# Two x loads moved to SyncE's queue, bands issued in order of use, a softmax planned later, five more evictions on ScalarE

## The chip, the cores and the metric

The kernel runs on one core of one Trainium2 chip. The metric is the device time in microseconds (us) of one execution. The core has five engines with a queue each: TensorE (PE, matmuls; PEld is its weight load), VectorE (DVE), ScalarE (ACT), GpSimd (POOL) and SyncE (SP). SP, ACT and POOL issue DMAs; "SPq" and "ACTq" are the queues of SP and ACT in the profile.

## The reference

All is float32. x has the shape 4 images x 256 channels x 64 x 64. First layer: attention over a dilated 7 x 7 neighbourhood; second layer: whitening of groups of 64 channels over all pixels of all images.

```python
k = conv(x, w1, rhs_dilation=(2, 2), padding=6) + b1          # 7x7, 256 -> 128
k = conv(k, w2, 1x1) + b2                                      # 128 -> 49
attn = softmax(k, axis=1)                                      # 49 weights per pixel
xp = pad(x, 6)
shifts = stack([xp[:, :, 2*u:2*u+64, 2*v:2*v+64] for u in range(7) for v in range(7)], 1)
y = einsum('bkchw,bkhw->bchw', shifts, attn)
# whitening: per group of 64 channels, mean and Sigma over all images and pixels,
# five Newton steps P = 1.5 P - 0.5 P^3 Sigma_N, then out = (P sqrt(rTr)) (y - mean) * weight + bias
```

## The kernel before, in words

**Storage.** x is kept in SBUF as "slots": slot k holds the rows of one parity of image k // 2 (k = 2b + parity). There are five SBUF buffers for eight slots. Slot 0 and 1 are loaded first in an order that suits the convolution of image 0 and later again in the order "halves" that the rest uses. `read_x` (L140) issues the four DMAs of one slot, 512 KB each, in runs of 32 floats; `load_x` (L158) calls it, or takes a copy arranged in DRAM beforehand (`ahead`, slots 5 to 7, one DMA of 2 MB). Results y overwrite x in the slots; `move` spills finished slots to DRAM and loads slots 5 to 7 in their place.

**Logits.** The two convolutions are merged and computed by a Toom-Cook scheme: seven row evaluations `br` and seven column points in three banks (`BANKS`). `conv_step(k, i)` runs the matmuls of bank i of row k (L599; 96, 80 and 32 of them), prepares the next row's inputs xh, rb, ct on DVE (L347, L350, L354) and fetches weights wr: by ACT's queue from DRAM (`wr<-gd`, L419), or, the first time a row is used, built from kept sums that SP loads (L428, L445) and stored again (L481). `direct_start`, `direct_inf` and `direct0` are the direct products (L765). Interpolation on DVE gives the logits.

**Softmax.** `soft(b, pc)` handles image b and column parity pc in two steps. Each turns half of the logits by PE transposes (L999); DVE takes maxima (L1035, L1036) and ACT does 16 exps with sums (L1039); the second step scales and shuffles on DVE (L1014 to L1023, four shuffles at L987) and marks the pair in `soft_done`. The second step is called after the next conv step (`rest_of`). The last image uses `softmax_rows` (L1060 to L1069), with more of it on DVE.

**Weighted sum.** The sum over the 49 shifts is done in 16 units n = 4b + k, one per image, row parity h and column parity pc. For one n: `move_terms(n)` (L1085) copies the softmax terms into a staging tile zt (11 copies, on ACT at L1117, for the last image on DVE at L1129) and writes it to DRAM scratch `sd` with eight DMAs (L1136, on POOL; four of n = 12 on SP). It returns without doing anything when the softmax of that pair isn't in `soft_done`. `load_band(n, half)` (L1162) reads from sd, by SP, the banded matrices of one half of the image: two DMAs `band` (L1173, column halves h0 and h1, 242 KB each) and two small ones `bandz` (L1184) for the edge between the halves. `first_half(n)` and `second_half(n)` turn x blocks by PE transposes (L1218, evicted by ACT at L1232 and L1241, in the tail by DVE), multiply them with the bands (L1269) in the order of `PIECES` (half 0 uses the mains first and the edge last; half 1 the edge first), and call `store_y` (L1287, L1289), which evicts the sum to the slot: the two channel halves cc = 0 and 1 both on ACT, but in the tail (`tail` set, from second_half(10) on) cc = 1 on DVE. `turn_y` transposes y (L1300, evicted at L1308), `moments` accumulates the statistics (L1321).

**Order of the work.** PE's order is the program's. A tile scheduler orders the other queues by its own estimates and priorities, subject to data dependencies and to manual ones: a "NoSync" dependency only fixes the order of two instructions, a "Sync" one makes the later wait. The weighted sums of image b are laid between the conv steps of image b + 1 or later. `plan(b, j, f)` puts f into eighth j of image b's conv steps (j of 8 and more goes on into the next image), in the order in which the calls were made, and `gap(b, j)` runs them. For image 1 the units start in eighth 2 of image 2: `first_half(4)` is planned for (2, 2), `second_half(4)` for (2, 3), `first_half(5)` for (2, 4), and so on; for image 2 `first_half(8)` comes at (3, 3). The softmaxes of images 1 and 2 are planned for eighths 0 and 1 of the next image, those of image 0 run at fixed places. `first_half(n)` itself calls `move_terms(n + 1)` and `load_band(n + 1, 0)` at its end; `second_half(n)` calls `bands(n + 1)`, which does for n + 1 (and the terms of n + 2) whatever is possible by then and hasn't been done.

**The x loads in question.** Slot 1 is loaded again (its second arrangement) after `load_band(0, 1)`, and slot 4 from the plan of eighth (1, 2); both on POOL's queue, eight DMAs in all, with a Sync dependency on the last DMA of band (0, 1) (`behind`, `first_band`).

Of the kernel before, what the change touches and what calls it, by code (L numbers as in the profile page):

```python
# [32 lines left out]
def kernel(  # L33
# [29 lines left out]
    nc = tc.nc  # L63
    B, C, H, W = x.shape
    P = 128
    NCC = C // P
# [3 lines left out]
    R = KS // 2  # L70
    SH, SW = H // 2, W // 2
    CR = P // SW
    NCH = SH // CR
    HALF = SH // 2
# [11 lines left out]
    TR8, TC = 8, SW // 2  # L86
    WS = 22
    TROWS = TR8 + R
    ROW0 = (0, TR8 - R, 2 * TR8, 3 * TR8 - R)
    COLS = ((0, TC + R), (TC - R, SW))  # L90
    LS = 2 * KS * WS
    RS = TC * (LS - 1) + WS
    HS = SH * RS
# [15 lines left out]
    def tp():  # L109
        return ps_tp.tile([P, 512], F32, tag="tp", name="tp")  # L110
# [18 lines left out]
    slots = {}  # L129
    store = []  # L130

    def halves(t):

        return t.rearrange("p c r w -> p c (r w)").rearrange(
            "p c (h r w) -> p c h r w", h=2, r=SH
        )

    ahead = {}

    def read_x(o, k, queue):  # L140
        b, pr = divmod(k, 2)
        dmas = []
        for cc in range(NCC):
            src = x[b, cc * P : (cc + 1) * P].rearrange("c (r two) w -> c r two w", two=2)
            for h in range(2):
                dmas.append(
                    queue.dma_start(o[:, cc, h], src[:, :, pr, h * SW : (h + 1) * SW])  # L147
                )
        return dmas

    def arrange_x(k, queue):

        ahead[k] = dram.tile([P, NCC * SH * W], F32, name=f"ahead{k}")
        return read_x(
            ahead[k].rearrange("p (c h r w) -> p c h r w", c=NCC, h=2, w=SW), k, queue
        )

    def load_x(s, k, queue):  # L158
        slots[k] = store[s]
        if k in ahead:  # L160
            return [queue.dma_start(store[s].rearrange("p c r w -> p (c r w)"), ahead[k])]
        return read_x(halves(store[s]), k, queue)

    s01 = ctx.enter_context(tc.tile_pool(name="s01", bufs=1))
    for s in range(2):
# [17 lines left out]
    t = tp()  # L183
# [3 lines left out]
    t = tp()  # L187
# [5 lines left out]
    for k in range(2):  # L193
        t = ps_cv.tile([P, 512], F32, name=f"cv{k}")
# [19 lines left out]
    for c0, c1 in ((0, 3), (3, 6), (6, 9), (9, 11), (11, 13)):  # L214
        c0, c1 = c0 * CB, min(c1 * CB, P)
# [32 lines left out]
    for k, c0 in enumerate(range(0, P, CB)):  # L248
        n = min(CB, P - c0)
        t = cv_buf[k % 2]  # L250
# [15 lines left out]
    for k0 in range(0, KT, TB):  # L266
        n = min(TB, KT - k0)
        t = tp()
# [622 lines left out]
    def behind(dmas, name):  # L891
        for dma in dmas:
            tc.add_manual_dep(
                dma.ins,
                name,
                mybir.DependencyInfo(mybir.DependencyClass.Sync, mybir.DependencyReason.DATA),
                reason="behind",
            )
# [14 lines left out]
    for s in range(2, 4):  # L913
        behind(load_x(s, s, nc.gpsimd), quiet)
# [10 lines left out]
    for k in range(5, 8):  # L925
        behind(arrange_x(k, nc.gpsimd), turn[0])
# [14 lines left out]
    )  # L941
    row_eval(0, 5, [rb[0], rb[1], xrs[5]])
    load_x(0, 0, nc.gpsimd)
    col_interp(0, 1)
    col_interp(0, 2)
# [23 lines left out]
    band = bpool.tile([P, 4, 2, TROWS, WS], F32, name="band")  # L969
    bandz = bpool.tile([P, 2, R, SW], F32, name="bandz")  # L970
# [56 lines left out]
    def softmax(b, pc):  # L1027

        nm = f"{b}_{pc}"
        mx = work.tile([P, NCH, 2], F32, tag="mx", name=f"mx_{nm}")  # L1030
        d = new_terms(b, pc)
        s = work.tile([P, 2, NCH], F32, tag="s", name=f"s_{nm}")
        for hf, t in enumerate(turned_logits(b, pc)):
            m = mx[:, NI * hf : NI * (hf + 1)]
            nc.vector.tensor_reduce(m, t[:, :, :, :KT], AX.X, ALU.max)  # L1035
            nc.vector.tensor_scalar(m, m, -1.0, None, ALU.mult)  # L1036
            for i in range(NI * hf, NI * (hf + 1)):
                for h in range(2):
                    nc.scalar.activation(  # L1039
                        d[:, h, i], t[:, i % NI, h, :KT], AF.Exp,  # L1040
                        bias=mx[:, i, h : h + 1], accum_out=s[:, h, i : i + 1],
                    )
            if hf == 0:
                yield
        for h in range(2):
            scale_terms(nm, h, d[:, h], s[:, h])
        shuffle(d.rearrange("p h i (u v) -> p (h i u) v", u=KS))
        soft_done.update((b, pc, h) for h in range(2))
# [23 lines left out]
        soft_done.add((b, pc, h))  # L1072

    terms, moved, loaded = {}, set(), set()
    written, soft_done, moved_by, first_band = [], set(), {}, []

    MOVES = [(0, 0, 4), (2, 0, 2), (2, 2, 2)]
    MOVES += [(s, j, 1) for s in (1, 3) for j in range(CR)]
# [72 lines left out]
    def bring_back(after):  # L1151

        for k in back:
            dma = nc.sync.dma_start(slots[k].rearrange("p a r w -> p (a r w)"), spill[k])
            tc.add_manual_dep(
                dma.ins,
                after.ins.name,
                mybir.DependencyInfo(mybir.DependencyClass.NoSync, mybir.DependencyReason.DATA),
                reason="bring_back",
            )  # L1160

    def load_band(n, half):  # L1162

        if (n, half) in loaded or n not in moved:
            return
        loaded.add((n, half))
        D = sd[n % 2][:]
        base = lambda t, h: (
            h * HS + TR8 * t * RS + (ROW0[t] - TR8 * t + R) * WS + COLS[h][0] - h * TC + R
        )  # L1170
        t0 = 2 * half
        for h in range(2):
            nc.sync.dma_start(  # L1173
                band[:, t0 : t0 + 2, h].rearrange("p t r w -> p t (r w)"),
                bass.AP(
                    tensor=D.tensor,
                    offset=D.offset + base(t0, h),
                    ap=[[LS - 1, P], [base(t0 + 1, h) - base(t0, h), 2], [1, TROWS * WS]],
                ),
            )  # L1180
        e = CR * half + (R if half else 0)
        for h in range(2):
            c0, c1 = COLS[h]
            dma = nc.sync.dma_start(  # L1184
                bandz[h * 64 : (h + 1) * 64, half, :, c0:c1],
                bass.AP(
                    tensor=D.tensor,
                    offset=D.offset + h * HS + (HALF - CR * half) * RS + e * WS + c0 - h * TC + R,
                    ap=[[LS - 1, 64], [WS, R], [1, c1 - c0]],
                ),  # L1190
            )
        if (n, half) == (4 * B - 1, 1):
            bring_back(dma)
        if (n, half) == (0, 1):
            first_band.append(dma.ins.name)
            behind(load_x(1, 1, nc.gpsimd), *first_band)

    blocks = {}

    tail, ahead_xb = [], []  # L1200
# [5 lines left out]
    def where(n):  # L1206

        b, h, pc = place(n)
        return slots[2 * b + h], pc
# [69 lines left out]
    def store_y(n, half):  # L1279
        yt, pc = where(n)  # L1280
        ps = y_ps.pop((n, half))
        for cc in range(NCC):
            o = halves(yt)[:, cc, :, half * HALF : (half + 1) * HALF, bass.ds(pc, TC, 2)]
            i = ps[:, cc].rearrange("p r (h c) -> p h r c", h=2)
            with tc.high_priority():
                if tail and cc:
                    nc.vector.tensor_scalar(o, i, pivot[:, cc : cc + 1], None, ALU.add)  # L1287
                else:
                    last = nc.scalar.activation(o, i, AF.Identity, bias=pivot[:, cc : cc + 1])  # L1289
        return last  # L1290
# [70 lines left out]
    def first_half(n):  # L1361
# [23 lines left out]
        weighted_sum(n, 0, 3)  # L1385
        weighted_sum(n, 0, 4)
        move_terms(n + 1, store_y(n, 0))
        half_done.add(n)
        load_band(n + 1, 0)
        if last is not None:  # L1390
            moments(last, 1)
# [5 lines left out]
    def bands(n, after=None):  # L1397

        move_terms(n, after)
        if n - 1 in half_done:  # L1400
            load_band(n, 0)
        if n - 1 in done:
            load_band(n, 1)
            move_terms(n + 1, after)
# [28 lines left out]
    def plan(b, j, *what):  # L1433
        todo.setdefault((b + j // NPC, j % NPC), []).extend(what)
# [3 lines left out]
    def soft(b, pc):  # L1438
        steps = softmax(b, pc)

        def step():
            with tc.high_priority() if pc == 0 else nullcontext():
                next(steps, None)

        step()
        if b == 0:
            step()
            if pc == 0:
                bands(0)
        else:  # L1450
            rest_of.append(step)
# [18 lines left out]
                    plan(b + 1, 3 + j, hs[j])  # L1470
    for b in range(B - 1):
        for j in range(2) if b else ():
            plan(b + 1, j, lambda b=b, j=j: soft(b, j))

    plan(1, 2, lambda: behind(load_x(4, 4, nc.gpsimd), *first_band))

    def gap(b, j):
        for f in todo.pop((b, j), ()):
# [2 lines left out]
    for b in range(1, B):  # L1481
# [13 lines left out]
        j, at, whole = 0, 0, sum(c for c, _ in steps)  # L1495
# [39 lines left out]
    n = 4 * last_b  # L1535
# [140 lines left out]
    n = [0]  # L1676
# [15 lines left out]
    for b in (3, 2, 1, 0):  # L1692
        for cc in range(NCC):
            for q in range(0, SH // TR, 2):
# [31 lines left out]
                for k in range(2):  # L1726
                    for i in (G0, G1):
                        o = i if k == 0 else (G1 if i is G0 else G0)
# [45 lines left out]
```

## Time and profile before

| | |
|---|---|
| time before, median of 3 runs | 729.38 us (725.12 to 730.21) |
| the profiled execution, its own time | 729.77 us |
| its span, first to last instruction | 727.8 us |
| mean granted clock of TensorE | 0.976 |
| PE busy | 687.1 us, 94% of the span |
| PEld, DVE, ACT, POOL busy | 543.5, 585.8, 341.5, 131.2 us |
| ACT L1289, y to slot, x53 | 0.735 us median of one |
| DVE L1287, y to slot, x11 | 0.751 us median of one |
| POOL L147, x load, x20 | 512 KB each, 7.5 us to landing (median) |
| SP L1173, band, x64 | 242 KB each, 3.2 us to landing (median) |
| POOL L1136, sd<-zt, x124 | 77 KB each, 3.0 us to landing (median) |

A line of the page's groups or of the timeline reads: source line, engine, operation, output<-inputs by the names of the program, shape, count, times. "Granted clock" is TensorE's clock as a share of full speed. A wait is written "who <- whom", with the sum in us, how often, and the longest. The chain of waits is the sequence of work and waits that ended last. The conv steps fill roughly 20 to 570 us, the weighted sums of the last image 570 to 660, the whitening matrix 660 to 673, and its application with the output stores the rest.

### The profile page before, as it was taken

How to read it: one execution, taken by the hardware profiler on the slowest of the kernel's cores; microseconds unless marked ns; L12 is line 12 of the kernel's file. 1: busy time of each engine (PE TensorE's matmuls, PEld its weight loads, DVE VectorE, ACT ScalarE, POOL GpSimd, SP SyncE). 2: the span in 40 equal slices, each digit the busy share in tenths (PEclk: the TensorE clock that was granted, in tenths of full speed). 3: DMA queues.
4: the chain of work that ended last, by engine and by line, in shares of the span. 5: the costliest groups of instructions: out<-in, count | busy, mean ns of one | idle time of the engine just before them, and what ended most of it. 6: DMA issues, size and time to landing. Idle time of an engine off the chain costs nothing.

```text
span 727.8 us, 19131 instructions
## 1 busy us (share of the span) xinstructions
PE 687.1 (94%) x7728; PEld 543.5 (75%) x7728; DVE 585.8 (80%) x1284; ACT 341.5 (47%) x954; POOL 131.2 (18%) x190
## 2 busy tenths in 40 slices
PE   6999999999998999998999999989999987997996
PEld 1449553377997998787999988889999877995231
DVE  3799998995796889999896699999969778325575
ACT  1423330133764565556563653646546533442564
POOL 0002625612361020002220200021302032200000
PEclk9999999999998999999999999999999999997998
DMA  8942999912897385226594760262733254463598
GB/s 324 233 122 94 240 386 216 228 30 56 220 239 208 115 261 198 92 63 166 170 308 132 235 203 2 62 178 81 194 103 66 59 126 97 108 247 145 237 361 326
DMA packets 78720, 126.09 MB, mean 173 GB/s; under 512 B 36471, under 2 KB 59112, under 8 KB 77480
## 3 DMA queue, kind: packets, MB, share of 16 engines
q1 hardware_dynamic: 60488, 64.84, 28.2%
q0 software_dynamic: 12096, 41.77, 21.7%
q10 hardware_dynamic: 6048, 18.27, 8.0%
q8 instruction: 61, 1.00, 0.6%
q14 instruction: 27, 0.22, 0.1%
HBM read 78.78 MB, written 52.36 MB: 180 GB/s over the span
## 4 chain that ended last, share of the span: by engine, by line
PE 69%; DVE 19%; ACT 5%; DMA 4%; issue 1%; SPq 0%; ACTq 0%; DVEq 0%
PE cv L599 21%; PE y L1269 10%; PE cv L765 9%; PE acc L765 8%; PE tp L1714 4%; PE tp L1300 4%; PE sig L1321 3%; PE tp L1218 3%; DMA band<-sd 3%; PE cv L253 2%; DVE pv L354 2%; DVE zz L354 2%; DVE d L987 1%; DVE xh L354 1%; DVE rb L347 1%
## 5 line engine op out<-in xcount | busy, mean ns | idle before, releaser
L599 PE MATMUL cv<-xh,wr 128*49 128x128 f32 x4160 | 232.4, 273 | 2.1 <-DMA wr<-gd 2.1
L599 PEld LDWEIGHTS cv<-xh,wr 128*49 128x49 f32 x4160 | 226.1, 124 | 5.8 <-issue 3.4
L1136 POOL DMA_DIRECT2D sd<-zt x124 | 65.3, 533 | 333.2 <-ACT zt L1117 272.7
L1269 PE MATMUL y<-band,xb 128*128 128x209 f32 x480 | 104.2, 349 | 7.1 <-DMA band<-sd 6.9
L1269 PEld LDWEIGHTS y<-band,xb 128*128 128x128 f32 x480 | 83.7, 196 | 8.2 <-DMA band<-sd 7.3
L610 ACT COPY pv<-cv 113x486 f32<-113x486 f32 (+2 forms) x60 | 25.9, 431 | 90.0 <-PE cv L599 83.0
L1308 ACT COPY yt<-tp 128x256 f32<-128x256 f32 x128 | 45.3, 377 | 41.7 <-PE tp L1300 40.8
L1300 PE MATMUL tp<-ident,slot 128*128 128x128 f32 x256 | 53.5, 306 | 8.7 <-DVE slot L1287 6.0
L354 DVE SCALAR_TENSOR_TENSOR pv<-pv 113x162 f32<-113x162 f32 x176 | 52.8, 321 | 4.2 <-ACT pv L610 3.4
L1300 PEld LDWEIGHTS tp<-ident,slot 128*128 128x128 f32 x256 | 41.4, 205 | 17.1 <-DVE slot L1287 6.7
L1218 PE MATMUL tp<-ident,slot 128*128 128x128 f32 x256 | 49.0, 305 | 3.3 <-ACT yt L1308 2.0
L1289 ACT ACTIVATE slot<-y,pivot 128x512 f32<-128x512 f32 x53 | 36.5, 736 | 25.7 <-PE y L1269 25.6
L147 POOL DMA_DIRECT2D slot<-in_x_dram x20 | 33.9, 1696 | 64.1 <-issue 50.5
L1218 PEld LDWEIGHTS tp<-ident,slot 128*128 128x128 f32 x256 | 38.6, 206 | 8.5 <-ACT xbz L1241 2.4
L1117 ACT COPY zt<-d 32x112 f32<-32x112 f32 (+2 forms) x132 | 38.3, 290 | 13.2 <-DVE d L987 11.3
L354 DVE SCALAR_TENSOR_TENSOR xh<-ct 128x512 f32<-128x512 f32 x40 | 26.7, 693 | 17.4 <-PE cv L599 17.3
L1232 ACT COPY xb<-tp 128x256 f32<-128x256 f32 x96 | 33.3, 375 | 14.2 <-PE tp L1218 13.4
L1321 PE MATMUL sig<-yt 128*64 128x65 f32 x1024 | 37.8, 228 | 0.0
L1321 PEld LDWEIGHTS sig<-yt 128*64 128x64 f32 x1024 | 33.3, 140 | 5.6 <-issue 4.0
L1039 ACT ACTIVATE d<-tp,mx 128x49 f32<-128x49 f32 x96 | 27.5, 322 | 20.9 <-DVE mx L1036 18.1
L765 PE MATMUL acc<-slot,tap 128*49 128x256 f32 (+7 forms) x224 | 34.7, 468 | 0.0
L765 PEld LDWEIGHTS acc<-slot,tap 128*49 128x49 f32 x224 | 16.2, 123 | 17.9 <-issue 15.5
(242 smaller groups left out, 1116.6 us busy)
## 6 DMA issues: line engine op xcount, KB each, us to landing
out_dram<-out SPq DMA_DIRECT2D x32, 512.0 KB, 3.6
band<-sd SPq DMA_DIRECT2D x64, 242.0 KB, 3.2
slot<-in_x_dram POOLq DMA_DIRECT2D x20, 512.0 KB, 7.5
sd<-zt POOLq DMA_DIRECT2D x124, 77.0 KB, 3.0
wr<-gd ACTq DMA_DIRECT2D x14, 588.0 KB, 5.5
wr<-gd ACTq DMA_DIRECT2D x14, 490.0 KB, 5.2
ahead<-in_x_dram POOLq DMA_DIRECT2D x12, 512.0 KB, 7.5
spill<-slot POOLq DMA_DIRECT2D x3, 2048.0 KB, 10.4
```

The lines of the kernel that those rows point to most:

```text
L147: queue.dma_start(o[:, cc, h], src[:, :, pr, h * SW : (h + 1) * SW])
L354: return in_turn(STT(o, a, f, b, ALU.mult, ALU.add))
L599: nc.tensor.matmul(o, wv[:, sc, sr, cc], xv[bc][:, h * NCC + cc], start=(j == 0), stop=(j == len(terms) - 1), skip_group_check=True,)
L765: nc.tensor.matmul(ps[h * HB : h * HB + KT, :, o0:o1], w[v][:, cc], rhs, start=(j == 0 and k == 0), stop=(j == len(order) - 1), skip_group ...
L1117: ins = nc.scalar.copy(o, i)
L1136: dma = queue.dma_start(bass.AP(tensor=D.tensor, offset=D.offset + h * HS + g * RS, ap=[[LS, TC], [CR * RS, NCH], [1, KS * WS]],), zt[p0 : ...
L1218: nc.tensor.transpose(t[:, cc * P : (cc + 1) * P], tile_of(xt, cc, t8, h, pc), ident)
L1269: nc.tensor.matmul(ps[:, cc, q0 : q0 + nq, c0:c1], xb[:, cc * P : (cc + 1) * P], rhs, start=(k == 0), stop=(k == len(PIECES[half]) - 1), s ...
L1289: last = nc.scalar.activation(o, i, AF.Identity, bias=pivot[:, cc : cc + 1])
L1300: nc.tensor.transpose(t[:, cc * P : (cc + 1) * P], tile_of(yt, cc, i // 2, i % 2, pc), ident,)
L1308: return nc.scalar.copy(yb.rearrange("p a g c -> p (a g) c")[:, :, :GW], t[:, :C].rearrange("p (e c) -> p e c", c=GW),)
L1321: nc.tensor.matmul(sig[g * GW : (g + 1) * GW, cc], yb[:, cc, g, :GW], yb[:, cc, g], start=(count[0] == 0 and cc == 0), stop=(count[0] == 4 ...
```

## The change

1. Slot 1 is loaded by SP's queue instead of POOL's, in order behind the last DMA of band (0, 1), without waiting for its landing.
2. Slot 4 is loaded by SP's queue, one DMA each in eighths 2, 3, 4 and 5 of image 1, after whatever else is planned for that eighth.
3. All band and bandz DMAs, and these x loads, are chained with NoSync dependencies in program order (`behind_band`); half 1 issues its edge DMAs ahead of its main ones.
4. The second softmax (pc = 1) of images 1 and 2 is planned for eighth 2 instead of eighth 1 of the next image.
5. cc = 1 is evicted by DVE only for n > 12, so that five evictions, of (10, half 1), (11, both halves) and (12, both halves), go to ACT.

```diff
     def read_x(o, k, queue):
         b, pr = divmod(k, 2)
-        dmas = []
         for cc in range(NCC):
             src = x[b, cc * P : (cc + 1) * P].rearrange("c (r two) w -> c r two w", two=2)
             for h in range(2):
-                dmas.append(
-                    queue.dma_start(o[:, cc, h], src[:, :, pr, h * SW : (h + 1) * SW])
-                )
-        return dmas
+                yield queue.dma_start(o[:, cc, h], src[:, :, pr, h * SW : (h + 1) * SW])
...
+    def behind_band(dma):
+        tc.add_manual_dep(
+            dma.ins,
+            last_band[0],
+            mybir.DependencyInfo(mybir.DependencyClass.NoSync, mybir.DependencyReason.DATA),
+            reason="behind_band",
+        ) if last_band else None
+        last_band[:] = [dma.ins.name]
...
+        for dma in (*edge(), *main()) if half else (*main(), *edge()):
+            behind_band(dma)
         if (n, half) == (4 * B - 1, 1):
             bring_back(dma)
         if (n, half) == (0, 1):
-            first_band.append(dma.ins.name)
-            behind(load_x(1, 1, nc.gpsimd), *first_band)
+            for dma in load_x(1, 1, nc.sync):
+                behind_band(dma)
...
-                if tail and cc:
+                if n > 4 * (B - 1) and cc:
                     nc.vector.tensor_scalar(o, i, pivot[:, cc : cc + 1], None, ALU.add)
                 else:
                     last = nc.scalar.activation(o, i, AF.Identity, bias=pivot[:, cc : cc + 1])
...
     for b in range(B - 1):
         for j in range(2) if b else ():
-            plan(b + 1, j, lambda b=b, j=j: soft(b, j))
-
-    plan(1, 2, lambda: behind(load_x(4, 4, nc.gpsimd), *first_band))
+            plan(b + 1, 2 * j, lambda b=b, j=j: soft(b, j))
+
+    slots[4] = store[4]
+    pieces = read_x(halves(store[4]), 4, nc.sync)
+    for j in range(2, 6):
+        plan(1, j, lambda: behind_band(next(pieces)))
```

`main()` and `edge()` are the two loops of `load_band` that issued the `band` and the `bandz` DMAs before, unchanged but for the `yield`.

More of the change, by code (lines that the diff above doesn't have):

```diff
@@ L145, in read_x @@
             for h in range(2):
-                dmas.append(
-                    queue.dma_start(o[:, cc, h], src[:, :, pr, h * SW : (h + 1) * SW])
-                )
-        return dmas
+                yield queue.dma_start(o[:, cc, h], src[:, :, pr, h * SW : (h + 1) * SW])
     def arrange_x(k, queue):
         ahead[k] = dram.tile([P, NCC * SH * W], F32, name=f"ahead{k}")
-        return read_x(
-            ahead[k].rearrange("p (c h r w) -> p c h r w", c=NCC, h=2, w=SW), k, queue
-        )
+        return [
+            *read_x(ahead[k].rearrange("p (c h r w) -> p c h r w", c=NCC, h=2, w=SW), k, queue)
+        ]
     def load_x(s, k, queue):
@@ L161, in load_x @@
             return [queue.dma_start(store[s].rearrange("p c r w -> p (c r w)"), ahead[k])]
-        return read_x(halves(store[s]), k, queue)
+        return [*read_x(halves(store[s]), k, queue)]
     s01 = ctx.enter_context(tc.tile_pool(name="s01", bufs=1))
@@ L1074 @@
     terms, moved, loaded = {}, set(), set()
-    written, soft_done, moved_by, first_band = [], set(), {}, []
+    written, soft_done, moved_by, last_band = [], set(), {}, []
     MOVES = [(0, 0, 4), (2, 0, 2), (2, 2, 2)]
@@ L1171, in load_band, with main, edge @@
         t0 = 2 * half
[L1172 to L1180, printed above, removed]
-        e = CR * half + (R if half else 0)
[L1182 to L1191, printed above, removed]
+        e = CR * half + (R if half else 0)
+        def main():
+            for h in range(2):
+                yield nc.sync.dma_start(
+                    band[:, t0 : t0 + 2, h].rearrange("p t r w -> p t (r w)"),
+                    bass.AP(
+                        tensor=D.tensor,
+                        offset=D.offset + base(t0, h),
+                        ap=[[LS - 1, P], [base(t0 + 1, h) - base(t0, h), 2], [1, TROWS * WS]],
+                    ),
+                )
+        def edge():
+            for h in range(2):
+                c0, c1 = COLS[h]
+                yield nc.sync.dma_start(
+                    bandz[h * 64 : (h + 1) * 64, half, :, c0:c1],
+                    bass.AP(
+                        tensor=D.tensor,
+                        offset=D.offset + h * HS + (HALF - CR * half) * RS + e * WS + c0 - h * TC + R,
+                        ap=[[LS - 1, 64], [WS, R], [1, c1 - c0]],
+                    ),
+                )
+        for dma in (*edge(), *main()) if half else (*main(), *edge()):
+            behind_band(dma)
         if (n, half) == (4 * B - 1, 1):
```

## Prediction

> **What bounds the kernel now.** I read the page's busy shares first: TensorE (PE) 687.1 of 727.8 us, DVE 585.8, ACT 341.5. PE is nearly full, so the change can only win where PE stands still or runs at a lowered clock, and a wait that it adds to PE is paid in full. So the next view is the list of what PE itself waited for (total, times, longest, us):
>
> ```profile
> PE y L1269 <- DMA band<-sd: 6.9, 2, 3.5
> PE tp L1300 <- DVE slot L1287: 6.0, 4, 2.8
> PE cv L599 <- DMA wr<-gd: 2.1, 1, 2.1
> ```
>
> The timeline of PE gives their places (start, duration, line, operation; output<-inputs, count); the last bracket is the idle time just before the line:
>
> ```profile
> 221.66 0.87 PE L1269 MATMUL y<-band,xb 128*128 128x209 f32 x4
> ...
> 226.79 1.76 PE L1269 MATMUL y<-band,xb 128*128 128x209 f32 x4 [3.54 <-DMA band<-sd]
> ...
> 343.61 0.98 PE L1269 MATMUL y<-band,xb 128*128 128x209 f32 x4 [3.35 <-DMA band<-sd]
> ...
> 592.92 1.75 PE L1300 MATMUL tp<-ident,slot 128*128 128x128 f32 x7 [1.33 <-DVE slot L1287]
> 594.60 2.00 PE L1321 MATMUL sig<-yt 128*64 128x65 f32 x32
> ```
>
> The same four matmuls take 0.87 us at 221.66 and 1.76 after the 3.54 us gap; the 32 sig matmuls take 1.15 elsewhere. A gap can cost twice: idle, then slow matmuls. The windows agree: granted clock 0.78 and 0.88 in 220 to 240, 0.83 to 0.93 in 590 to 620, 1.00 nearly everywhere between.
>
> Why was the band late at 226.79? SyncE's queue, then POOL:
>
> ```profile
> 210.11 0.37 SPq L1173 DMA_DIRECT2D band<-sd  x1
> 210.60 1.15 SPq L1184 DMA_DIRECT2D bandz<-sd  x1
> 211.85 1.15 SPq L1173 DMA_DIRECT2D band<-sd  x2
> ```
> ```profile
> 206.95 5.07 POOL L147 DMA_DIRECT2D slot<-in_x_dram  x3 [0.70 <-DMA sd<-zt]
> 215.08 1.68 POOL L147 DMA_DIRECT2D slot<-in_x_dram  x1 [3.07 <-issue]
> ```
>
> first_half(1) (n=1) needs both band pieces of its half. The one that PE waited for was the third band DMA on SP (212.64), behind one of the other half, and it took 14.1 us by the chain of waits (median of all bands 3.2) beside four 512 KB x loads. At 343.61 the order is the same (third band, issued 337.28, 6.3 us), with no x load near.
>
> **What the Trainium skill says.** "TensorE: Matmul & The Clock Gate", part 1: an idle window of about 3.4 us halves PE's clock until a busy one has passed. The trace agrees in size (0.87 to 1.76), not as a sure threshold: 3.35 us at 343.61 cost nothing more. "DMA: Bandwidth & Descriptors", Queues, rings and completion order: the 16 DMA engines take turns between queue rows, and within a row take descriptors in ring order; so x on another queue shares with a band, x behind it on the same queue comes later. The 14.1 us agree with the first half; no run shows the second. Same page, Anatomy of one DMA: a wait is made on the issuing sequencer; so a waiting DMA holds all behind it. SP's row shows a bandz issue stretching 6.57 us from 215.22.
>
> **A. x loads and band order, image 0.** Eight x DMAs (slots 1 and 4, 512 KB each) leave POOL, where each took 1.69 us to issue, and go to SP: four behind band (0,1) at about 186, where SP is empty until 210; then one each in eighths 2 to 5 of image 1, each behind the band just issued. Band (1,0) h1 becomes the second DMA. Gone: 3.54 idle plus the slow clock. From the late band to the end of bandz first_half(1) took 6.18 (226.79 to 232.97); the same products in first_half(2) take 4.05 (267.68 to 271.73), 3.55 without two waits of together 0.5. Of the 2.6 between, some 0.3 are two transposes more: 2.3 us of slow clock. A = -5.8, bounds -6.5 and 0. Slot 4 is first read at 271.2 (ACT L506); the last piece goes out behind band (2,1), near 252, and needs 5 to 8 us to land: covered by about 10 us of conv, beyond which each us late counts.
>
> **S. The price on SP.** An x row is 32 floats, 128 B, so 4096 runs per DMA. Nearest row: 16 HWDGE loads of 256 KB in 256 B runs, 1.14 us median to issue. By bytes 2.3 us, by runs 4.6. Queued behind pieces and waiting bands are the weight loads of L428 and L445 (rb<-g5d issued 221.89 and first used by DVE at 248.2; wr<-g4d issued 223.2, used by PE at about 241 with 4.2 us landing: some 12 us to spare, 6 if PE is 6 earlier). Gain excluded, loss 0 to 8; I take +1.0.
>
> **B. Order at n=4.** h1 goes out at about 335.3 instead of 337.28. From 334.78 to 343.57 three band DMAs (256 runs of 968 B each) and two bandz (192 short runs each) went; in the new order only two bands stand up to h1's end. By bytes 8.8 x 484/754 = 5.6 us, by runs 8.8 x 512/1152 = 3.9: landing at 338.7 to 340.4, and PE asks at 340.3. The wr loads beside it stay. B = -3.0 of 3.35, at worst 0.
>
> **C. soft(1,1) an eighth later.** It is now planned behind first_half(4) in the same gap, so move_terms(5), called inside first_half(4), finds soft_done empty and returns; it runs at the end of second_half(4) instead. In the old times: y ends 364.8; two evictions on ACT to 366.1; 11 zt copies of 0.29 with two xb copies to 370.1; eight sd DMAs on POOL of 0.53, from 369.5 to 373.8; landing 1.4 (as from 333.43 to band at 334.78); band 3.6: 378.8. PE has 7.1 us of conv (128 matmuls) and reaches first_half(5)'s band at 374.9. A new stall of 3.9, with half the 2.3 slow clock: C = +5.1. At best (no contention) +2, at worst (the spill and slot loads of 2 MB beside it, as band took 14) +11. Its own gain: 32 exp steps of ACT and 3 us of shuffle leave the stretch before 338; a 0.92 PE wait moves along, 0.
>
> **D. soft(2,1) later.** Its exps stand ahead of the wr load on ACT: conv bank 0 ended 477.1, the load went out 478.51, landed 485.3, PE waited 2.12; the transposes waited 1.07. Moved to 481, the exps run before first_half(8), whose 7 us give slack. move_terms(9) comes later still. D = -2.1, bounds -3.2 and +2.
>
> **E. Evictions of five halves, (10,1) to (12,1), cc=1.** DVE L1287 is 0.75, ACT L1289 0.735, five times: equal work. Even an idle DVE starts its half just when ACT has done (21.9 us, 7 times, DVE slot waiting for ACT slot), so nothing parallel is lost. But DVE ran it late behind shuffles and zt copies: 584.52 instead of 582.6, 592.11, 607.03. PE stalls 1.62, 1.33, 0.80 and 2.82 = 6.57; of the last two about 1.5 stay (two ACT evictions with no PE work between). The slow clock adds 0.85 (sig) + 0.34 + 0.47 (L999) + 0.42 + 0.75 + 0.24 = 3.1. Limit -8.2. DVE is busy 33 of 40 us there and then becomes the limit, with DVE's own terms for n=13 to 15; I take -6.0, lower bound -3.
>
> **Sum.** -5.8 + 1.0 - 3.0 + 5.1 - 2.1 - 6.0 = -10.8. The profiled execution was 729.77 (span 727.8, 2.0 around it, unchanged), so 719.0; the median shown, 729.38, is 0.4 less: 718.6. A measurement tells about 1% (7.3 us) from no change.
>
> **Rivals.**
> *R1, the new wait eats it:* C reaches 9 to 11 under contention and E only 3 to 4. -5.8 + 1 - 3 + 10 - 2.1 - 3.5 = -3.4: 726. For: band 14.1 us once; sd landings up to 10.2. Against: the spill, now bound behind an earlier sd, starts earlier.
> *R2, C hidden:* zt and sd go quickly, C +2 without slow clock, E -8, S 0: -16.9 and 712.5. For: PE's stall of 3.35 had no slow clock. Against: the sum of C has few soft terms.
> *R3, slower:* SP's queue becomes the bound. A band that waits for PE, with an x piece behind it, holds the first weights of rows 4, 5 and 0 (L445). Free up to 6 us of holding; to turn -10.8 into +8 it must hold about 12 in each of the three rows: 19/3 + 6. Time 738. For: SP waits of PE for bands go to 12.1 us. Against: pieces follow bands, and most loads have slack.
> *R4, the x loads only collide elsewhere:* unpacked 128 B runs at 4.6 us spoil band (1,1) or (2,0) as they did (1,0): A falls to -1: 723.5. Against: the bands stand ahead on the same queue.
>
> **Chances.** Forecast (714.5 to 722) 0.42; R1 0.26; R2 0.18; R3 0.09; R4 0.05. Range 709 to 731 leaves out R3 and the tails; the likeliest alone is 714.5 to 722. Faster by over 1% (below 722.1): 0.42 + 0.18 + a little of R4 = 0.62; within 1%: 0.28; slower: 0.10.
>
> **What would show it.** A right: no PE wait for band near 222, clock 1.00 there. B: at n=4 main bands first and second, wait under 1. C: a PE wait for band of about 4 at first_half(5), sd for n=5 after the evictions of second_half(4). D: no wait for wr near 485. E: L1287 x6 and L1289 x58, no PE wait for DVE slot before first_half(13). Wrong if SP's weight loads release PE or DVE (R3), or if C is nil or doubled.

## The result, and the profile after

The kernel after takes 734.21 us (median of 6 runs, 733.39 to 735.37) against 729.19 (725.12 to 730.46, 6 runs) before: ratio 1.0081, 95% interval 1.0054 to 1.0109. It is slower by 0.8%, where 1.5% faster was forecast, and the time lies above the range. The span is 732.0 us, the mean granted clock 0.973 (before 0.976).

The list of PE's own waits has changed as the change intends in two of its three rows: `wr` is gone, and the DVE slot wait went from 6.0 to 0.2 us. The first row more than doubled:

```profile
PE y L1282 <- DMA band<-sd: 15.6, 2, 8.2
...
PE tp L1313 <- DVE slot L1300: 0.2, 1, 0.2
```

The timeline of PE says where. The wait of first_half(1), at 226.79 before, has gone (the first three lines are its matmuls now); the one of first_half(4), at 343.61 before, has grown from 3.35 to 8.16, and first_half(5) has one that wasn't there:

```profile
221.75 0.87 PE L1282 MATMUL y<-band,xb 128*128 128x209 f32 x4
223.17 0.88 PE L1282 MATMUL y<-band,xb 128*128 128x209 f32 x4
225.12 1.58 PE L1282 MATMUL y<-band,xb 128*128 128x209 f32 x8
...
339.56 1.76 PE L1282 MATMUL y<-band,xb 128*128 128x209 f32 x4 [8.16 <-DMA band<-sd]
...
382.43 1.76 PE L1282 MATMUL y<-band,xb 128*128 128x209 f32 x4 [7.47 <-DMA band<-sd]
```

Both gaps are followed by four matmuls in 1.76 us instead of 0.87, so each is paid in idle time and again in slow matmuls. To see where time was won and lost I took from both timelines the moment at which PE starts the sig matmuls (the statistics, `moments`) within a half (us; the difference is after minus before, cumulative):

| start of sig in | before | after | difference |
|---|---|---|---|
| first_half(1) | 232.97 | 228.08 | -4.9 |
| second_half(3) | 322.59 | 317.40 | -5.2 |
| first_half(4) | 347.07 | 346.38 | -0.7 |
| second_half(4) | 364.76 | 365.33 | +0.6 |
| first_half(5) | 379.78 | 389.91 | +10.1 |
| second_half(7), the last of image 1 | 465.84 | 475.98 | +10.1 |
| first_half(8) | 501.59 | 508.76 | +7.2 |
| first_half(13) | 621.36 | 623.79 | +2.4 |
| end of the span | 727.8 | 732.0 | +4.2 |

So the x loads and the band order won 5.2, the softmax of image 2 3.0, the evictions 4.7; first_half(4) lost 4.5 where a gain of 3.0 was forecast, first_half(5) lost 9.6 (forecast 5.1). The loss at n = 4 is the surprise: there the band is issued in the new order, main DMAs first. The timeline of POOL's queue shows what is new beside it, first before, then after:

```profile
351.74 1.05 POOL L1136 DMA_DIRECT2D sd<-zt  x2 [18.31 <-ACT zt L1117]
...
356.72 0.57 POOL L1339 DMA_DIRECT2D spill<-slot  x1
```
```profile
323.98 4.29 POOL L1132 DMA_DIRECT2D sd<-zt  x8 [54.26 <-ACT zt L1113]
328.26 0.57 POOL L1352 DMA_DIRECT2D spill<-slot  x1
...
370.06 4.31 POOL L1132 DMA_DIRECT2D sd<-zt  x8 [24.85 <-ACT zt L1113]
374.64 4.30 POOL L1132 DMA_DIRECT2D sd<-zt  x8 [0.27 <-ACT zt L1113]
```

The spill of slot 1 (2 MB) starts 28 us earlier, 3 us ahead of the first band of n = 4, for which PE now waits:

```profile
331.17 2.32 SPq L1182 DMA_DIRECT2D band<-sd  x2
```

Two lines of the kernel explain it: `first_half(4)` calls `move_terms(5)` and then `move(1)`, and `move` orders its spill behind `written[0]`, the last sd DMA issued. Since soft(1, 1) now comes after first_half(4), `move_terms(5)` returns at once, `written[0]` is still that of n = 4, and nothing holds the spill behind the terms of n = 5.

### The profile page after: what moved, and what is told of

The parts are those of the page before. It is cut to its first block, busy times and chain, and to the rows that moved or that the text cites. A ratio compares the mean times of both kernels' runs of the same rounds, so it can differ in the third digit from the quotient of the medians.

```text
span 732.0 us, 19143 instructions
## 1 busy us (share of the span) xinstructions
PE 686.5 (94%) x7728; PEld 541.5 (74%) x7728; DVE 583.1 (80%) x1279; ACT 344.9 (47%) x959; POOL 117.6 (16%) x182
## 4 chain that ended last, share of the span: by engine, by line
PE 55%; DVE 20%; issue 13%; DMA 5%; ACT 5%; POOL 1%; SPq 0%; ACTq 0%; DVEq 0%; POOLq 0%
PE cv L595 15%; PE cv L761 8%; PE acc L761 8%; PE y L1282 7%; PE tp L1730 4%; PE tp L1313 3%; PE sig L1334 2%; PE tp L1231 2%; DVE pv L350 2%; DVE xh L350 2%; PE cv L249 2%; DVE zz L350 2%; DMA spill<-slot 1%; DVE rb L350 1%; PE apply L1746 1%
## 5 line engine op out<-in xcount | busy, mean ns | idle before, releaser
L1302 ACT ACTIVATE slot<-y,pivot 128x512 f32<-128x512 f32 x58 | 39.6, 735 | 24.4 <-PE y L1282 24.3
L1245 ACT COPY xb<-tp 128x256 f32<-128x256 f32 x96 | 33.4, 376 | 24.7 <-PE tp L1231 23.9
L346 DVE TENSOR_TENSOR pv<-pv 113x162 f32<-113x162 f32 (+1 forms) x77 | 27.9, 373 | 0.4
```

The lines of the kernel that those rows point to most:

```text
L1245: (nc.vector.tensor_copy if n >= 4 * (B - 1) else nc.scalar.copy)(xb, t[:, :C])
```

## Experiments

The kernel before ran beside them each time (medians 728.9 to 729.65). The theory under test is the last paragraph: the later softmax lets the spill out beside the band of n = 4, and makes the terms of n = 5 late. The main rivals are that the wait at n = 4 comes from the new band order, or from the order of PE's work, and that the time is lost by the x loads on SP.

**1. The softmax put back.** All of the change but its point 4.

```diff
-            plan(b + 1, 2 * j, lambda b=b, j=j: soft(b, j))
+            plan(b + 1, j, lambda b=b, j=j: soft(b, j))
```

> The changed kernel with only the softmax plan put back to eighths 0 and 1. Theory (the late softmax leaves move_terms(5) undone in first_half(4); that makes the terms of n=5 late, and lets the spill of slot 1 go out right behind the terms of n=4, into band (4,0)): both new PE waits go, at n=4 (8.16 us in the changed kernel) under 1 us, at n=5 (7.47 us) nil; the spill is issued behind the terms of n=5; the waits before the wr load near image 3 come back (+3). Time 716 to 719. Rival (the chained band and x order on SP causes the wait at n=4): a wait of 6 us or more stays at n=4, time 723 to 727.

720.91 us (719.25 to 723.29), ratio 0.9895 (0.9861 to 0.993). No wait at n = 5; at n = 4 it is 2.08, so the "under 1" missed, and the time is a little over the range given. That wait is for the second band; PE needed the first at 333.27 and found it landed. POOL's queue, and PE:

```profile
345.06 4.29 POOL L1132 DMA_DIRECT2D sd<-zt  x8 [17.06 <-ACT zt L1113]
349.34 0.57 POOL L1352 DMA_DIRECT2D spill<-slot  x1
```
```profile
336.93 0.98 PE L1282 MATMUL y<-band,xb 128*128 128x209 f32 x4 [2.08 <-DMA band<-sd]
```

With the terms of n = 5 back in first_half(4), the spill is back behind them. The other four points together make the kernel 1% faster; the softmax plan costs 13 us beside them.

**2. The softmax alone**, and **3. the softmax of image 2 alone.** The first is the kernel before with only the plan of point 4; the second is the kernel after with the plan changed for image 2 only.

```diff
+            plan(b + 1, 2 * j, lambda b=b, j=j: soft(b, j))     # 2, on the kernel before
+            plan(b + 1, j * b, lambda b=b, j=j: soft(b, j))     # 3, on the kernel after
```

> The kernel before with only the softmax plan moved (second softmax of images 1 and 2 in eighth 2). Theory: the two waits appear without any of the other edits: about 8 us at n=4 and 7 at n=5, each with slow matmuls after it; 3 us come back at image 3. Time 736 to 740. Rival (SP order causes it): n=4 as in the kernel before (3.4), only n=5 late; time 731 to 735.

743.57 us (743.45 to 744.92), ratio 1.0208 (1.0178 to 1.0237), some 4 us more than expected. The band waits were 5.15 (n = 1), 8.88 (n = 4) and 8.73 (n = 5), with the spill at 334.85, again early. So the loss at n = 4 appears with the old band order as well: the new order isn't its cause.

> The changed kernel with the later softmax for image 2 only; image 1 has its own back in eighth 1. Theory: no new wait at n=4 and n=5, and the gain of 3 us at image 3 (wr load not behind the exps) stays: 713 to 716, 3 below soft_back. If moving image 2's softmax gains nothing by itself, it equals soft_back.

717.63 us (716.11 to 718.46), ratio 0.9841 (0.9806 to 0.9875): 3.3 below the first experiment, as said, though both lie higher than expected. The later softmax of image 2 is a gain, that of image 1 the whole loss.

**4. The spill late, the softmax still moved.** `move(1)` is called at the end of second_half(4), behind its `bands(5)`.

```diff
-            if last % 2:
+            if last % 2 and last != 3:
                 move(last // 2)
...
         bands(n + 1, last)
+        if n == 4:
+            move(1)
```

> The changed kernel with the move of slot 1 (spill, and the load into its place) called at the end of second_half(4), behind the terms of n=5 and 6, instead of in first_half(4). The softmax stays late. Theory (two separate costs): the wait at n=4 falls from 8.16 to under 1.5 us and the slow matmuls after it go; the wait at n=5 stays, 6 to 9 us. Time 724 to 728. Rival (only the lateness of the terms counts and the spill is innocent): n=4 keeps its 8 us, time 733 to 735.

729.82 us (726.62 to 733.36, 20 runs), ratio 1.0007 (0.9993 to 1.0021), above the range given. The wait at n = 4 fell from 8.16 to 4.71, not below 1.5, and n = 5 kept its wait (7.80):

```profile
PE y L1282 <- DMA band<-sd: 12.5, 2, 7.8
```
```profile
376.59 0.58 POOL L1352 DMA_DIRECT2D spill<-slot  x1 [1.28 <-DMA sd<-zt]
```

So the spill isn't all of the wait at n = 4. The band that PE waits for is the first of n = 4, as in the kernel after. PE asks for it at 331.5 (its start less its wait) where it came to it at 333.3 in experiment 1, because the eight softmax transposes (some 2 us with their wait) have left the stretch ahead. And the band is issued 2.3 us later, at 331.65 against 329.35, the sd writes ahead of it taking 2.6 to 4.8 us to land instead of 2.8 to 3.2. Beside them ACT now issues a `wr` load at 326.62 that went out at 330.71 in experiment 1, when the exps stood before it. The kernel after (load at 326.46, band at 331.17) and experiment 6 (326.68 and 331.71) show the same pair. That this load delays the sd writes is argued from the order of the two, not isolated.

**5. The spill early, the softmax not moved.** The counterpart: the first experiment, with the spill issued ahead of the terms of n = 5.

```diff
-        move_terms(n + 1, store_y(n, 0))
+        stored = store_y(n, 0)
+        if n == 4:
+            put_away(1)          # the spill of move(1), taken out of it
+        move_terms(n + 1, stored)
```

> The kernel after with the second softmax of each image back in the eighth behind the first (as in soft_back) and one more edit: the spill of slot 1 is issued ahead of the terms of n = 5, so right behind the terms of n = 4, where the kernel after has it, while the softmax and all else stay as in soft_back. Nothing is left out. Theory, that in the kernel after the 2 MB spill beside band (4,0) is what holds first_half(4): the spill starts within 5 us of the band's issue, the wait for the band at n = 4 rises from the 2.1 us of soft_back to 5 to 8 us, TensorE is slow behind it, there is still no wait at n = 5, and the time is 724 to 728 us. Rival, that the wait at n = 4 comes of PE's order (softmax transposes moved) and of the band's late issue, not of the spill: the wait at n = 4 stays at 2 to 3 us and the time at 719 to 722 us.

728.95 us (726.35 to 730.95, 20 runs), ratio 0.9998 (0.9981 to 1.0015), a little over the range given and 8 us above the first experiment by the medians (5.4 by the two profiled executions, of which experiment 1's is the slowest of its four). POOL's queue, and PE:

```profile
323.77 4.29 POOL L1132 DMA_DIRECT2D sd<-zt  x8 [53.75 <-ACT zt L1113]
328.05 0.58 POOL L1358 DMA_DIRECT2D spill<-slot  x1
```
```profile
340.34 1.76 PE L1282 MATMUL y<-band,xb 128*128 128x209 f32 x4 [6.86 <-DMA band<-sd]
```

SP issues the first band at the same time, within 0.01 us, in experiment 1 and here:

```profile
329.35 1.58 SPq L1182 DMA_DIRECT2D band<-sd  x2
```
```profile
329.34 2.12 SPq L1182 DMA_DIRECT2D band<-sd  x2
```

The summary of the band's tile in 327 to 342 gives the time from issue to landing of the second band, first in experiment 1, then here:

```profile
DMA to landing us min/median/max: 6.3/6.3/6.3
```
```profile
DMA to landing us min/median/max: 10.7/10.7/10.7
```

The first band, which had landed within 3.9 us in experiment 1 (PE used it at 333.27), is the one that PE waits for here, and the chain of waits gives it 10.96:

```profile
329.34 10.96 DMA band<-sd
```

The stretches of the two (us; busy time of PE, PEld, DVE, ACT and POOL; granted clock; DMA share; GB/s), again 1 and then 5:

```profile
330.00:340.00 10.00, 7.92 (x86) 7.48 (x81) 10.00 (x23) 7.58 (x31) 0.00 (x0) 1.00 0.77 217
340.00:350.00 10.00, 10.00 (x185) 9.72 (x185) 8.43 (x22) 6.61 (x18) 4.76 (x9) 1.00 0.32 76
```
```profile
330.00:340.00 10.00, 3.48 (x56) 3.10 (x52) 10.00 (x23) 4.44 (x21) 0.00 (x0) 0.93 0.99 353
340.00:350.00 10.00, 9.66 (x80) 9.06 (x82) 3.84 (x15) 5.56 (x16) 0.55 (x1) 0.73 0.53 155
```

With the spill the DMA engines are full (0.99, 353 GB/s), the second band takes 4.4 us longer and the first at least 7, PE waits 4.8 longer, and the clock is 0.73 just when PE has work again. From the sig matmuls of second_half(3) to those of first_half(4) it is 23.2 us in experiment 1 and 30.4 here: in this kernel the place of this one DMA costs 7.1 us on the path. The rival of experiment 5 falls, and the theory stands for n = 4, with PE's earlier arrival and the later issue of the band as its second part.

**6. The softmax early enough for the terms of n = 5.** The kernel after, with soft(1, 1) still in eighth 2 of image 2, but both its steps ahead of first_half(4).

```diff
+    todo[2, 2].insert(0, todo[2, 2].pop())
...
-        if b == 0:
+        if b == 0 or (b, pc) == (1, 1):
             step()
```

> The changed kernel with soft(1,1) still in eighth 2 of image 2, but with both of its steps ahead of first_half(4) instead of behind it, so that soft_done is set when first_half(4) calls move_terms(5). Theory (the place within the gap does the harm, not the eighth): no wait for a band at n=5, spill behind the terms of n=5, wait at n=4 of 2 to 5 us; 716 to 721. Rival (in eighth 2 the softmax itself is too late for n=5 whatever the order): n=5 keeps 4 us or more, 724 to 732.

723.27 us (721.69 to 723.54), ratio 0.9921 (0.9889 to 0.9952), above what was expected. The wait at n = 5 is gone and the spill is late, as the theory says, but first_half(4) gets other waits. PE's timeline:

```profile
334.49 1.55 PE L1282 MATMUL y<-band,xb 128*128 128x209 f32 x4 [1.19 <-DMA band<-sd]
...
339.01 0.70 PE L1231 MATMUL tp<-ident,slot 128*128 128x128 f32 x2 [2.55 <-ACT xbz L1254]
...
342.95 0.70 PE L1231 MATMUL tp<-ident,slot 128*128 128x128 f32 x2 [0.56 <-ACT d L1035]
```

The exps stand on ACT just ahead of the evictions that PE waits for, and the clock is 0.74 to 0.75 in 330 to 350. So neither of the two places tried in eighth 2 is good: ahead of first_half(4) the exps come with 5.5 us more than in experiment 3 between the sig matmuls of second_half(3) and first_half(4), and behind it they delay the terms.

**7. The other parts alone.** Each is the kernel before with one part: the evictions; the band chain and order, with x left on POOL; the x loads on SP, with the bands not chained and in the old order.

```diff
-                if tail and cc:
+                if n > 4 * (B - 1) and cc:
...
+        for dma in (*edge(), *main()) if half else (*main(), *edge()):
+            behind_band(dma)
...
+            for dma in load_x(1, 1, nc.sync):
+                behind_band(dma)
```

> The kernel before with only the eviction edit (cc = 1 of five halves on ScalarE instead of VectorE). Theory (DVE ran those evictions late behind its softmax work): the PE waits for DVE slot (6.0 us before) fall under 1 us, the slow matmuls near 595 and 608 go, 4 to 5 us of gain: 724 to 726. Rival (VectorE's own softmax chain is the bound of that stretch and only the releaser's name changes): under 1.5 us of gain, 728 to 730.

725.6 us (723.5 to 727.85, 14 runs), ratio 0.9947 (0.9929 to 0.9964): inside, and PE's wait for the DVE slot is down to 0.2.

> The kernel before with only the chaining of the band DMAs in program order (edge first in half 1); x loads stay on POOL, softmax and evictions as before. Theory (the order alone makes the h1 band second instead of third): the wait of 3.54 at first_half(1) shrinks to 0 to 2 although the x loads still run beside, n=4 falls from 3.35 to about 2: 723 to 727. Rival (the x loads beside are the cause): first_half(1) keeps 3 us or more, time 727 to 729.

721.64 us (720.61 to 724.37), ratio 0.9899 (0.9854 to 0.9943): better than expected, as the wait at first_half(1) went entirely; at n = 4 it is 1.62.

> The kernel before with only the x loads of slots 1 and 4 moved to SP behind bands; the bands themselves are not chained to each other. Theory (order matters more): the h1 band stays third, but without x loads beside it lands in time: the wait at first_half(1) goes (under 0.5), n=4 keeps about 3.4: 723 to 726. Rival (SP's queue pays for the x loads: weight loads late): a new PE or DVE wait for wr or rb between 230 and 270, time 728 or more.

726.14 us (724.06 to 730.32, 20 runs), ratio 0.9955 (0.9938 to 0.9972), just over the range given; the wait at n = 4 is 2.65 instead of 3.4. Here too the wait at first_half(1) went: either part alone was enough. The tile's summary for the four bands of n = 1 (205 to 222) tells why, in turn before, with the bands alone, and after:

```profile
DMA to landing us min/median/max: 11.1/14.1/14.6
```
```profile
DMA to landing us min/median/max: 7.4/9.1/10.8
```
```profile
DMA to landing us min/median/max: 3.6/3.9/4.0
```

With x on SP, in order with the bands, they land in 4 us. With x still beside them they need 9, but the one that is needed goes out second instead of third, and that was in time, though with nothing to spare, as the next experiment shows.

**8. The best of it.** Bands chained and ordered, evictions on ACT, the later softmax for image 2 only, x on POOL as before.

> The kernel before with the chain and order of the band loads, the last sums evicted on ScalarE and the later second softmax for image 2 alone; the x loads of slots 1 and 4 stay on POOL as before. Nothing is left out. If the x loads' move to SyncE is worth nothing once the bands are ordered, as bands_only and x_only beside soft_back suggest, it takes 716 to 719 us, as soft_img2 did (717.6), with no wait for a band at first_half(1) and one of 1.5 to 2.5 us at n = 4. If the x move has a worth of its own (POOL's queue is held by the 2 MB of x), it is 720 to 724 us, with a wait for a band at first_half(1) or at n = 4 over 3 us.

717.75 us (716.74 to 718.84), ratio 0.9838 (0.9791 to 0.9885): as experiment 3 (717.63), which has x on SP. In detail the expectation missed: a band wait of 2.16 remains at first_half(1), where the bands alone had none; the first band goes out at 212.12 here and went out at 210.28 there. The sig matmuls there start 2.5 us later than in experiment 3. By the last sig matmuls 0.3 of it is left (645.67 against 645.33). So moving x is worth 2.5 us locally, and no gain was measured in the end. Both versions beat the kernel before by 1.6% and, by the medians, the kernel after by 2.3%.

## Why the prediction was wrong, point by point

**What bounds the kernel** was right: the two large losses are PE stalls behind a DMA, and both were paid again in slow matmuls.

**A and S** (-5.8 and +1.0, so -4.8) came to -4.9 at first_half(1) and -5.2 by second_half(3). The feared hold of SP's queue (R3) didn't come: four x loads took 12.64 us to issue back to back, but at 186 to 199 where nothing needed the queue, the single ones 0.57 to 0.61, and no weight load released PE late. One reading under that fear was loose: the row of 6.57 us from 215.22 is two bandz issues, of 1.87 and 0.58 us, with 4.1 us between them, and not one long issue.

**B** (-3.0, "at worst 0") is the step that failed. It took the traffic beside the band of n = 4 as unchanged but for the bands themselves ("The wr loads beside it stay"), and C put the departure of the softmax from that stretch at 0. From second_half(3)'s sig to first_half(4)'s it is 24.5 us before; the runs split the change like this:

| | us | change |
|---|---|---|
| before | 24.5 | |
| experiment 1: new order, softmax in its old place | 23.2 | -1.3 |
| experiment 4: softmax moved, spill late | 25.2 | +2.0 |
| kernel after: softmax moved, spill early | 29.0 | +3.8 |

The order gave less than half of the forecast, as the second band still took 6.3 us to land (with the bands alone, in experiment 7, the stretch is 22.7, so -1.7). The 2.0 come with PE's earlier arrival and the band's later issue (experiment 4), and the 3.8 with the place of the spill; where the softmax stays, that place costs 7.1 (experiment 5), so it has no single price. I had read in the diff that the spill would go behind an earlier sd write; under R1 I booked it as an argument against a loss ("starts earlier"), because it would be out of the way of n = 5. I didn't ask what it would then lie beside: the band of n = 4, on a wait that my own list showed. Nor were the transposes saved: from first_half(4)'s sig to second_half(4)'s the kernel after takes 1.3 us more.

**C** (+5.1) was right in mechanism and place, and wrong in size: +9.6. PE reached the band at 374.96 (374.9 predicted), and the terms went out from 370.06 (369.5). What was too small was above all the band's landing. It was issued 1.9 us after the last of the eight sd issues had ended (374.37), where I had 1.4, and took 6.11 us, where I had 3.6:

```profile
376.28 6.11 DMA band<-sd
```

Eight more sd writes, those of n = 6, are issued beside it from 374.64; that they slow it is likely but was not isolated. I took both durations from quieter places, though my upper bound (+11) used a busier one. 4 us of idle time became 7.5, and with that the slow clock, which I had counted at half, came in full.

**D** (-2.1) gave -3.0, and the wait for `wr` is gone. **E** (-6.0) gave -4.7; from first_half(8)'s sig to first_half(13)'s the eight kernels with these evictions took 2.9 to 4.8 us less than before, so -6.0 was too much. Two new waits show a part of why: 1.61 us at 599.86 and 1.69 at 618.29, both for DVE evictions of x (L1245), which fits the fear that DVE becomes the limit there.

**The end.** From first_half(13)'s sig to the end of the span it is 108.2 us against 106.4. All of it lies behind the last sums: from the last sig matmuls to the end it is 71.1 against 69.4. Most of it, 1.4 us, is PE running slow for longer in the first output products, between two groups of `apply` matmuls; before, then after:

```profile
675.18 1.58 PE L1730 MATMUL apply<-slot,full 64*64 64x512 f32 x8
676.69 1.98 PE L1714 MATMUL tp<-slot,full 128*128 128x512 f32 x4
```
```profile
677.61 1.99 PE L1746 MATMUL apply<-slot,full 64*64 64x512 f32 x8
679.52 2.99 PE L1730 MATMUL tp<-slot,full 128*128 128x512 f32 x4
```

The three kernels with neither the band chain nor the x move have 106.4 to 106.6 from first_half(13)'s sig on, the nine others 106.9 to 108.5. Why full speed comes back later, and whether it is chance, stays open.

Summed from the profiles: -5.2 + 4.5 + 1.3 + 9.6 - 3.0 - 4.7 + 1.8 = +4.3, against +4.2 by the spans. Of the rivals R1 came nearest: its kind was right, a new wait that takes more than was won, but it had one such wait and there were two.

## What to carry to other kernels

When a step is moved past another, list not only what waits for it but also what is merely ordered by it: a call that returns early changes what "the last write" means for every later transfer that is queued behind that write. A large transfer that starts earlier isn't a gain by itself; look at what PE waits for in the stretch where it will now lie. And take the landing of a DMA in a new place from the busiest neighbouring stretch, not from the median, if PE will stand behind it.

## What the runs showed of the hardware

- A 2 MB spill on POOL's queue went with a stretch of a 242 KB band on SP's queue, issued 3.0 us behind it, from 6.3 to 10.7 us; the band before it, issued 1.3 us behind the spill, went from at most 3.9 to 11.0 (experiments 1 and 5). "DMA: Bandwidth & Descriptors", Queues, rings and completion order, in the Trainium skill, says that each DMA engine serves the queues that have work for it by turns; the runs agree that the two share, and show that sharing with a large neighbour isn't free for the small one.
- In most runs single gaps of 1.26 to 3.35 us left the next four matmuls at 0.98 us, and gaps of 3.54, 4.49 and more gave 1.76. This lies close to the idle window of about 3.4 us in "TensorE: Matmul & The Clock Gate", part 1, but it is no sure threshold in these runs: in experiment 8 a single gap of 2.16 us was followed by four matmuls in 1.44, and in experiment 6 one of 1.19, with one of 0.46 1.7 us ahead of it, by four in 1.55, at a clock of 0.74 in 330 to 340.

```profile
225.37 1.44 PE L1283 MATMUL y<-band,xb 128*128 128x209 f32 x4 [2.16 <-DMA band<-sd]
```

- Four x loads of 512 KB in runs of 128 B took 12.64 us of SP's queue back to back: the first 0.59, the three behind it 5.56, 3.50 and 2.85. Single ones with nothing of their kind ahead took 0.57 to 0.61. Why the later ones take longer isn't shown.
